# Where a graph layer's "own row" part is finished: at the first stage's store, or after the neighbour sums

## The chip, the cores and the metric

The kernel runs on one core of one Trainium2 chip. The metric is the device time of one launch in microseconds (us). The core has five engines that run side by side, each with its own in-order queue: TensorE (PE, with its weight loads shown as PEld), VectorE (DVE), ScalarE (ACT), GpSimd (POOL) and SyncE (SP, which here only issues transfers). They wait for each other through semaphores.

## The reference, cut to what matters

Four graph layers follow one another on x of 2708 x 512 numbers, each as `x = layernorm(x + layer(x, adj))`. The change touches the first layer alone:

```python
Ab   = A > 0                                   # A: 2708 x 2708
keep = Ab & (cumsum(Ab, axis=1) <= 64)         # the first 64 neighbours of each row
cnt  = keep.sum(axis=1, keepdims=True)
nb_mean = (keep @ X) / maximum(cnt, 1)
xj = leaky_relu(nb_mean @ W_nb.T + b_nb)       # neighbour part
xi = leaky_relu(X @ W_line.T + b_line)         # own part
out = xi + where(cnt > 0, xj, 0)
x1 = layernorm(x + out)                        # x of the next layer
```

The kernel computes `keep @ (X W_nb.T)` in place of `(keep @ X) W_nb.T`. leaky_relu is `max(0.01 u, u)`.

## The kernel before, in words

The 2708 rows are cut into 22 tiles: 21 of 128 rows and a last one of 20. A tile of x is 128 x 512 fp32, 256 KB.

**First stage** (the loop `for t in range(NT)`, up to 187 us in the profile). For each tile t, PE multiplies x(t), transposed, with W_nb (the first four matmuls of L299) and with W_line (the second four), two passes each. ACT and DVE split the first product into two parts, yH (L271) and yL (L276), whose sum the later matmuls use. DVE adds the bias to the second product (L451, tile `u`) and POOL issues the store of it to the array `r0_dram` (L452). So `r0_dram` holds `X W_line.T + b_line`, before the leaky step. The loads of x go over SP's queue (`fetched`, L205) into three buffers named `rows`; `early(k, ...)` issues them k tiles ahead of use.

Woven into the same loop is the work on 14 of the 22 row blocks of the adjacency: POOL issues the load of a block (L312, 677 KB), ACT counts its ones (L317, a sigmoid over 2708 columns), DVE finds the first 64 of each row in two parts, each a scan (L323) and a product (L326), and the block is then turned: every second one by a transposing transfer over SP's queue (L344) whose result ACT turns into the stored mask (L349), the others by PE (L335, ACT L339). `tc.issue_after(ins)` puts the instructions of its block behind `ins` on that engine: the load of the next adjacency block is put behind the store of the tile before (`stored[t - 1]`), the second part of `place` behind `low`, the last DVE instruction of the tile. The matmuls and transposes of this loop stand in a fixed order on PE (`pe`). The products lie in PSUM: one buffer each for `pm0` and `pm1`, and four buffers `acc` that the turning shares with every second product.

**Among the sums** (187 to 467 us). The tiles are summed in six groups, `cuts`: first the last two tiles (20, 21), then four at a time. For a group, PE runs over the 22 row tiles j (L608: the mask block kT times yH(j), yL(j)). kT is made by ACT one step ahead (L470, two buffers). ACT then scales the four sums into `u` (L621). The rest of a group is the generator `finish`, which is advanced during the next group's sums at the steps j that 3 does not divide (14 of 22), and in the last group's case once for each tile of the following loop. It adds the bias (L524), takes the leaky step (L229), fetches r0 and x (two `rows` buffers), takes the leaky step on r0 (L229 again, tile `rows`) and adds x (L528), adds the two parts (L530), normalises (L121 to L128, with one POOL instruction, L126), stores x1 (L532), and splits it into 16-bit words (L149, `store_words`) that are stored (L150) so that transposing transfers can load them turned (L155). The eight remaining adjacency blocks are counted, placed in four parts each (`other_masks`), and turned by L344 into ACT's L349 during the same sums, as steps of the generator `both`; they use the tiles `spare` and `w` in turn.

**The next layer's products** (467 to 625 us) repeat the first stage's pattern on x1: matmuls L299, yH, yL, bias add L642, and the mask rewritten by L636.

A scheduler orders the instructions of each engine, within the constraints named; SP's and POOL's queues are ordered by it too.

Of the kernel before, what the change touches and what calls it, by code (L numbers as in the profile page):

```python
# [16 lines left out]
OP = mybir.AluOpType  # L17
# [15 lines left out]
def kernel(  # L33
# [18 lines left out]
    def rows(t):  # L52
        return min(P, N - t * P)
# [183 lines left out]
    with ExitStack() as phase:  # L237
# [118 lines left out]
        with ExitStack() as ph:  # L356
            st = ph.enter_context(tc.tile_pool(name="l0a", bufs=1))
            wnT, wlT = weight(), weight2
            room = [maskT[:, G + k, :4 * D].bitcast(F32) for k in range(2 * KD)]

            fetches = []
            xs = early(2, NT, lambda t: fetched(x, t, rows(t), log=fetches))
            xTs = early(0, NT, lambda t, order=as_it_comes: transposed(ahead, ps_tr, xs(t), rows(t), "xT", order))

            warm = sums()
            for _ in range(8):
                pe(nc.tensor.matmul(warm[:, :P], ones, ones, start=True, stop=True))
            first_weights = list(transpose_weight(room[:KD], ps_tr, wnT, l0_w_nb, (nc.sync, nc.scalar)))  # L370
            line_weights = transpose_weight(room[KD:], ps_tr, wlT, l0_w_line)
            lows = {}
            xT = xTs(0, order=pe)
            lows[0] = keep_y(0, P, product(xT, P, wnT, 0, pe))
            xT = xTs(1, order=pe)
            weights_made = [next(line_weights) for _ in range(2)][0]
            pm = product(xT, P, wnT, 0, pe, sums())
            with tc.issue_after(list(line_weights)[-1].ins):
                lows[1] = keep_y(1, P, pm)
            b_line = bias(bcast(l0_b_line, D))  # L380
            def mask_tile():
                return st.tile([P, NT * P], BF16, name="m", bufs=3)

            def mask_rows(i):
                m = mask_tile()
                if i < 3:
                    with tc.issue_after(weights_made.ins):
                        nc.vector.memset(m[:, (0 if rows(turns[i]) < P else N - 1):], 0.0)
                else:
                    nc.gpsimd.memset(m[:, N:], 0.0)  # L390
                return load_mask(i, m)

            def by_dma(i):
                return i % 2 == 0 and i < HERE - 2

            def turned_tile():
                return end_tile(BF16)[:, :NT * P].rearrange("p (t n) -> p t n", n=P)

            masks = early(1, HERE, mask_rows)
            intos = {}  # L400

            def turn_next(i):
                if not by_dma(i):
                    for _ in turn_here(i, masks(i), lambda: sums(BF16, (P, G, P)), pe):
                        pass
                    return
                assert len(intos) < 2
                intos[i] = turned_tile()
                with tc.issue_after(fetches[-1].ins):
                    turn(i, masks(i), intos[i])  # L410
                due.append((t + 2, i))

            def signs_of(i, t):
                with tc.issue_after(highs[t].ins):
                    for _ in signs(i, intos.pop(i)):
                        pass
            masks(0)
            nc.gpsimd.memset(maskT[:, NT - 1, :], 0.0)
            nc.gpsimd.memset(maskT[:, :, N:], 0.0)
            counted = turned = 0  # L420
            due, stored = [], {}
            for t in range(NT):
                n = rows(t)
                if t == END:
                    assert not due and turned >= HERE - 2
                    ends[:] = [end_tile(F32R) for _ in range(2)]
                    for y in (yH, yL):
                        nc.gpsimd.memset(y(LAST).bitcast(F32), 0.0)
                if t > 1:

                    lows[t] = keep_y(t, n, product(xTs(t, order=pe), n, wnT, 0, pe, sums() if t % 2 else None))
                xT = xTs(t)
                if t + 1 < NT:
                    xTs(t + 1, order=pe)
                while due and due[0][0] <= t:
                    signs_of(due.pop(0)[1], t)
                while turned < min(HERE, counted - (t + 2 < NT and not by_dma(turned))):
                    turn_next(turned)
                    turned += 1
                now = counted < min(HERE, -(-t * HERE // (NT - 4)))  # L440
                if now:
                    with tc.issue_after(stored[t - 1].ins) if t > 2 else nullcontext():
                        m = masks(counted)
                    places = st.tile([P, N // 2], BF16, name="places", bufs=1)
                    with tc.issue_after(highs[t].ins), tc.issue_after(copied[0].ins):
                        count(counted, m)
                    with tc.issue_after(lows[t].ins):
                        place(counted, m, places, 0, 2)
                pm = product(xT, n, wlT, 1, pe, None if t % 2 else sums())
                u = sm.tile([P, D], F32, name="u")  # L450
                low = nc.vector.tensor_add(u[:n], pm[:n], b_line[:n])  # L451
                stored[t] = nc.gpsimd.dma_start(r0_dram[t * P:t * P + n, :], u[:n])  # L452
                if now:
                    with tc.issue_after(low.ins):
                        place(counted, m, places, 1, 2)
                    counted += 1
            with tc.issue_after(stored[LAST].ins):
                twins(0, turns[HERE - 1] + 1)
                twins(turns[0], NT)
# [3 lines left out]
        with ExitStack() as ph:  # L463
# [54 lines left out]
                nc.vector.reciprocal(one, one)  # L518

            def finish(ts_, us):  # L520
                for t in ts_:
                    n, u = rows(t), us[t]
                    r0, x0 = fetched(r0_dram, t, n), fetched(x, t, n)
                    nc.vector.tensor_add(u[:n], u[:n], b_nb[:n])  # L524
                    leaky(u[:n], u[:n])
                    with tc.issue_after(low.ins):
                        leaky(r0, r0)
                        nc.vector.tensor_add(r0, r0, x0)  # L528
                    yield
                    nc.vector.scalar_tensor_tensor(u[:n], u[:n], has[:n, t:t + 1], r0, op0=OP.mult, op1=OP.add)  # L530
                    layer_norm(sm, u[:n], n, u[:n])
                    nc.gpsimd.dma_start(x1_dram[t * P:t * P + n, :], u[:n])  # L532
                    store_words(r0 if ts_ == range(*cuts[-1]) else words, x1_words, t, u)
                    yield

# [1100 lines left out]
```

## Time and profile before

| what | us |
| --- | --- |
| median of 3 runs | 2882.63 (2882.36 to 2885.61) |
| the profiled execution | 2884.27 |
| its span from first to last instruction | 2882.5 |
| PE busy in it | 2806.0 (97%) |
| DVE busy | 2008.4 (70%) |
| ACT busy | 1525.4 (53%) |
| POOL busy | 267.1 (9%) |

The profile is one execution. A line such as "L608 PE MATMUL acc<-yH,kT" names the source line, the engine, the operation and the tiles, output first. "Idle before" is time in which the engine stood still just before that instruction, with what released it. The times of the timeline count from the start of the span. One instruction's time includes its latency: two instructions of one engine can overlap by a little, so the distance from start to start is what a further instruction costs on a busy engine. PEclk is the granted TensorE clock, 1.0 being full speed.

### The profile page before, as it was taken

The numbers are of one execution on the slowest core, as the hardware profiler recorded it, in microseconds if no ns is written. First come the engines' busy times: TensorE is split into PE (matmuls) and PEld (weight loads), VectorE is DVE, ScalarE is ACT, GpSimd is POOL, SyncE is SP. The second block draws the span as 40 slices with busy tenths as digits, with TensorE's granted clock in tenths as the row PEclk, the third lists the DMA queues.
The fourth block names the chain that finished last, engine by engine and source line by source line (L and its number), as shares of the span: only waits on it lengthen the run. The fifth ranks groups of instructions, "written<-read, shape, count | busy, mean of one in ns | idle before, by whom it ended". The sixth has DMA issues, their size and how long they took to land. (4 is left out here: it accounts for less than half of the span.)

```text
span 2882.5 us, 35707 instructions
## 1 busy us (share of the span) xinstructions
PE 2806.0 (97%) x13910; PEld 1553.3 (54%) x13910; DVE 2008.4 (70%) x2386; ACT 1525.4 (53%) x1749; POOL 267.1 (9%) x436
## 2 busy tenths in 40 slices
PE   9999999999999999999999999999999999999998
PEld 5457665458887433444466433444375555555565
DVE  7867747543436999999978999999954435445242
ACT  4646533223335999999955999999951000000011
POOL 2112110111110000000021000000200010100001
PEclk9999999999999999999999999999999999999999
DMA  7746647424323011111152111111161000000000
GB/s 172 154 98 135 148 128 189 129 76 123 106 87 75 28 37 37 35 55 38 36 167 94 38 38 41 50 42 34 36 162 62 4 26 15 26 15 16 15 15 28
DMA packets 203668, 202.64 MB, mean 70 GB/s; under 512 B 126837, under 2 KB 151738, under 8 KB 203490
## 3 DMA queue, kind: packets, MB, share of 16 engines
q1 hardware_dynamic: 170646, 127.60, 16.7%
q0 software_dynamic: 21840, 68.46, 8.1%
q10 hardware_dynamic: 11004, 4.22, 0.6%
q8 instruction: 111, 1.82, 0.3%
q14 instruction: 67, 0.55, 0.1%
HBM read 137.90 MB, written 55.66 MB: 67 GB/s over the span
## 5 line engine op out<-in xcount | busy, mean ns | idle before, releaser
L866 DVE SCALAR_TENSOR_TENSOR e<-v_bc,ucol,maskT 128x1408 f32<-128x1408 f32 (+3 forms) x798 | 1132.5, 1479 | 316.4 <-PE pn L1267 308.4
L895 ACT ACTIVATE c<-e,bcol 128x1300 fp8e4<-128x1300 f32 (+2 forms) x688 | 956.5, 1412 | 61.6 <-DVE e L866 16.2
L1067 PE MATMUL po<-e,R 128*64 128x512 f32 (+3 forms) x4224 | 894.0, 548 | 25.4 <-DVE e L866 23.1
L1067 PEld LDWEIGHTS po<-e,R 128*64 128x64 f32 (+1 forms) x4224 | 333.9, 136 | 552.5 <-issue 389.4
L1267 PE MATMUL pn<-e,R 128*128 128x512 f32 (+1 forms) x1008 | 396.3, 557 | 0.7
L1267 PEld LDWEIGHTS pn<-e,R 128*128 128x128 f32 x1008 | 177.5, 190 | 195.9 <-issue 181.2
L1196 ACT ACTIVATE w<-pl,b 128x256 f32<-128x256 f32 (+1 forms) x88 | 41.0, 466 | 365.6 <-PE pl L1194 365.6
L126 POOL TENSOR_TENSOR ln_rs<-ln_rs,half 128x1 f32<-128x1 f32 (+1 forms) x88 | 54.3, 617 | 1320.3 <-DVE ln_rs L125 1311.3
L608 PE MATMUL acc<-yH,kT 128*128 128x512 f32 x418 | 169.9, 407 | 5.7 <-ACT kT L470 4.8
L787 PE MATMUL pm<-w,xT 128*128 128x264 f32 (+1 forms) x704 | 164.0, 388 | 4.1 <-DVE R L805 1.5
L608 PE MATMUL acc<-yL,kT 128*128 128x512 f32 x418 | 163.4, 391 | 0.0
L658 PE MATMUL acc<-yH,mf 128*128 128x512 f32 x418 | 162.7, 389 | 0.0
L658 PE MATMUL acc<-yL,mf 128*128 128x512 f32 x418 | 162.6, 389 | 0.0
L1194 PE MATMUL pl<-lin 128*128 128x256 f32 (+1 forms) x704 | 152.9, 371 | 0.6 <-DVE lin L1096 0.6
L1219 PE MATMUL pl<-lin,w 128*128 128x512 f32 x336 | 150.8, 593 | 0.0
L1194 PEld LDWEIGHTS pl<-lin 128*128 128x128 f32 x704 | 129.3, 190 | 31.2 <-issue 15.8
L787 PEld LDWEIGHTS pm<-w,xT 128*128 128x128 f32 (+1 forms) x704 | 129.7, 190 | 29.7 <-ACT xT L141 4.2
L655 ACT CAST mf<-maskT 128x1024 fp32r<-128x1024 fp8e4 (+1 forms) x66 | 64.5, 978 | 148.5 <-PE acc L658 143.9
L299 PE MATMUL pm<-w,xT 128*128 128x512 f32 x288 | 130.1, 594 | 3.5 <-DVE yL L276 2.7
L470 ACT ACTIVATE kT<-maskT 128x512 fp32r<-128x512 fp8e4 (+1 forms) x132 | 77.6, 593 | 99.0 <-PE acc L608 98.8
L967 PE MATMUL pd<-c,parts_c 128*12 128x384 fp8e4 (+2 forms) x2688 | 128.3, 307 | 0.0
L299 PE MATMUL pm<-weight,xT 128*128 128x512 f32 (+1 forms) x256 | 117.1, 600 | 1.5 <-DVE u L642 1.5
(280 smaller groups left out, 2773.4 us busy)
## 6 DMA issues: line engine op xcount, KB each, us to landing
v_bc<-v_dram SPq DMA_DIRECT2D x16, 704.0 KB
rows<-in_x_dram SPq DMA_DIRECT2D x42, 256.0 KB
x_dram<-u POOLq DMA_DIRECT2D x42, 256.0 KB, 2.6
v_bc<-v_dram SPq DMA_DIRECT2D x16, 650.0 KB
m<-in_adj_dram POOLq DMA_DIRECT2D x13, 677.0 KB, 7.7
r_dram<-u POOLq DMA_DIRECT2D x21, 256.0 KB, 3.6
rows<-r_dram SPq DMA_DIRECT2D x21, 256.0 KB
z_dram<-u POOLq DMA_DIRECT2D x21, 256.0 KB, 2.6
```

The source lines that it names most:

```text
L299: order(nc.tensor.matmul(pm[:m], xT[:, k, :m], w[:, k, :], start=(k == 0), stop=(k == KD - 1)))
L470: made = nc.scalar.activation(kT[:, :w], maskT[:, j, b[0] * P:b[0] * P + w], AF.Relu, scale=-1.0)
L608: nc.tensor.matmul(pa[t], kT[:, (t - b[0]) * P:(t - b[0] + 1) * P], y(j), start=(j == 0 and y is yH), stop=(j == LAST))
L658: nc.tensor.matmul(pa, mf[:, j - g0, :], y(j), start=(j == 0 and y is yH), stop=(j == LAST))
L787: nc.tensor.matmul(pm[a][:m, :D // 2 + heads], xT[:, k, :m], w[:, k, a, :D // 2 + heads], start=(k == 0), stop=(k == KD - 1))
L866: self.made = nc.vector.scalar_tensor_tensor(e[:, :w], v[:, :w], ucol[:, j, h:h + 1], maskT[:, j, c0:c0 + w], op0=OP.max, op1=OP.mult)
L895: nc.scalar.activation(c[:, :w], e[:, :w], AF.Sigmoid, bias=bcol[:, j, h:h + 1], scale=STEP, saturate=False)
L967: pe(nc.tensor.matmul(p[32 * g:32 * g + 12, :c1 - c0], parts_c[:, j, h, :], c[:, c0:c1], start=(i == 0 and h == hs[0]), stop=(i == NT - 1 ...
L1067: pe(nc.tensor.matmul(po[i][HO * k:HO * k + HO, :c1 - c0], R2[at, j, h * HO:(h + 1) * HO], e[at, a:a + c1 - c0], start=(i_ == 0), stop=(i_ ...
L1194: nc.tensor.matmul(pl[:, :w], self.lin1[:, k, f * P:(f + 1) * P], h[:, k, :w], start=(k == 0), stop=(k == KD - 1))
L1219: nc.tensor.matmul(pl[:n], gT[:, f, (t - t0) * P:(t - t0) * P + n], self.lin2[:, f, :], start=(f == 0), stop=(f == KF - 1))
L1267: nc.tensor.matmul(pn[k][:, :w], R2[at, j, k * P:(k + 1) * P], e[at, :w], start=(j == 0), stop=(j == NT - 1))
```

## The change

In the first stage, the leaky step is taken on `u` right after the bias add, on DVE, in place; POOL adds the tile of x to it; then it is stored. So `r0_dram` holds `x + leaky_relu(X W_line.T + b_line)`. `low` now names the leaky step. The x tile is used once more, after its transposition, and the loads of x are issued one tile ahead of `xs` in place of two.

In `finish`, x is no longer fetched, and the leaky step on r0 and the add of x (L528) are gone. r0 is fetched one tile ahead within the group. The instruction that adds the two parts comes under `issue_after(low.ins)`, after a `yield`; and there is a third `yield` in each tile, between the normalisation with its store and `store_words`. A group of four tiles thus takes 12 steps where it took 8. In the last group the words are written into the r0 tile, as before.

```diff
-            xs = early(2, NT, lambda t: fetched(x, t, rows(t), log=fetches))
+            xs = early(1, NT, lambda t: fetched(x, t, rows(t), log=fetches))
...
                 u = sm.tile([P, D], F32, name="u")
                 low = nc.vector.tensor_add(u[:n], pm[:n], b_line[:n])
+                low = leaky(u[:n], u[:n])
+                nc.gpsimd.tensor_add(u[:n], u[:n], xs(t))
                 stored[t] = nc.gpsimd.dma_start(r0_dram[t * P:t * P + n, :], u[:n])
...
             def finish(ts_, us):
-                for t in ts_:
-                    n, u = rows(t), us[t]
-                    r0, x0 = fetched(r0_dram, t, n), fetched(x, t, n)
+                r0s = early(1, len(ts_), lambda i: fetched(r0_dram, ts_[i], rows(ts_[i])))
+                for i, t in enumerate(ts_):
+                    n, u, r0 = rows(t), us[t], r0s(i)
                     nc.vector.tensor_add(u[:n], u[:n], b_nb[:n])
                     leaky(u[:n], u[:n])
+                    yield
                     with tc.issue_after(low.ins):
-                        leaky(r0, r0)
-                        nc.vector.tensor_add(r0, r0, x0)
-                    yield
-                    nc.vector.scalar_tensor_tensor(u[:n], u[:n], has[:n, t:t + 1], r0, op0=OP.mult, op1=OP.add)
+                        nc.vector.scalar_tensor_tensor(u[:n], u[:n], has[:n, t:t + 1], r0, op0=OP.mult, op1=OP.add)
                     layer_norm(sm, u[:n], n, u[:n])
                     nc.gpsimd.dma_start(x1_dram[t * P:t * P + n, :], u[:n])
+                    yield
                     store_words(r0 if ts_ == range(*cuts[-1]) else words, x1_words, t, u)
                     yield
```

## The prediction

> **What bounds the kernel now.** PE is busy 97% of the span, so only its idle time and its clock can move the end. I cut the part that the change touches by stage (the table of windows; columns: time and, for PE, PEld, DVE, ACT and POOL, us busy and instructions; then PEclk, DMA share, GB/s):
>
> ```profile
> 28.40:95.00 66.60, 62.95 (x224) 30.93 (x223) 62.72 (x50) 37.84 (x53) 8.82 (x18) 0.97 0.72 149
> 95.00:169.50 74.50, 74.06 (x274) 37.09 (x273) 63.61 (x51) 46.16 (x60) 11.29 (x23) 1.00 0.68 143
> 169.50:187.40 17.90, 17.90 (x67) 7.80 (x65) 4.05 (x7) 5.06 (x10) 2.94 (x7) 1.00 0.34 83
> 187.40:219.00 31.60, 25.26 (x96) 16.60 (x96) 20.46 (x22) 17.22 (x31) 3.65 (x9) 1.00 0.42 93
> 219.00:467.00 248.00, 238.67 (x963) 178.74 (x964) 159.71 (x264) 124.67 (x190) 44.92 (x71) 0.98 0.57 144
> 467.00:535.00 68.00, 63.69 (x145) 26.70 (x144) 57.30 (x91) 15.74 (x19) 12.30 (x21) 1.00 0.61 170
> ```
>
> In the first 67 us of the adjacency work DVE idles 3.9 us, less than anything beside PE: it is as full as PE. From 187 us it is not. Then the waits, for what PE lost: of PE before 187 us (first line), of PE from 187 to 535 us (next three), of ACT among the sums (last); columns: total us, times, longest.
>
> ```profile
> PE acc L335 <- DVE u L451: 3.6, 1, 3.6
> ...
> PE acc L608 <- ACT kT L470: 13.1, 12, 3.3
> PE pm L299 <- DVE yL L276: 2.7, 2, 2.3
> PE pm L299 <- DVE u L642: 1.5, 1, 1.5
> ...
> ACT maskT L349 <- DMA weight<-spare: 12.4, 3, 5.1
> ```
>
> PE's one long stall of the first stage (at 89.4 us) is DVE's backlog: the buffer that PE needs was read by L451 only after a scan. Among the sums, three of PE's twelve stalls are long: 2.75 us at 216, 2.23 at 300, 3.30 at 347. Each time ACT had no kT ready because it stood, in order, behind L349, which waited 3.2, 4.1 and 5.1 us for a turned adjacency block. That transfer starts when DVE ends the block's last L326.
>
> Two of these stalls cost more than their gap (windows around 347, 300 and 89 us):
>
> ```profile
> 343.00:354.00 11.00, 7.70 (x22) 5.14 (x20) 8.47 (x14) 7.26 (x12) 0.53 (x1) 0.69 0.45 156
> 296.00:306.00 10.00, 7.56 (x25) 5.28 (x24) 6.66 (x7) 5.97 (x10) 1.45 (x3) 0.83 0.67 155
> 86.00:97.00 11.00, 7.57 (x19) 3.58 (x19) 9.23 (x7) 4.96 (x8) 1.36 (x4) 0.84 0.53 114
> ```
>
> Clock lost, (1 - PEclk) x window: 11 x 0.31 = 3.4 us, 10 x 0.17 = 1.7, 11 x 0.16 = 1.8. At 216 us nothing was lost.
>
> **What the Trainium skill says.** (1) "TensorE: Matmul & The Clock Gate", section "What's actually happening": after an idle window of about 3.4 us TensorE falls to half speed, and needs a busy window to return. The trace agrees on the loss (1.7 us is half of 3.4), but a gap of 2.23 us was enough. (2) "GPSIMD Engine Reference", section 8, "Key points": GpSimd shares its SBUF interfaces with VectorE, "contention with DVE instructions in a 2-port perf mode or with two SBUF inputs". (3) Same page, section 3.1: a GpSimd add of two tensors takes about twice VectorE's time. On (2) and (3) the trace has a case, the same kind of add late in the kernel (timeline of POOL, of DVE there, of DVE elsewhere; columns: start, us):
>
> ```profile
> 2644.34 1.30 POOL L1190 TENSOR_TENSOR rows<-rows,b 128x512 f32<-128x512 f32 x1
> ...
> 2644.55 1.64 DVE L1244 SCALAR_TENSOR_TENSOR acc<-e,ecol,acc 128x512 f32<-128x512 f32 x1
> ...
> 2568.93 0.75 DVE L1244 SCALAR_TENSOR_TENSOR acc<-e,ecol,acc 128x512 f32<-128x512 f32 x1
> ```
>
> The add takes 1.30 us (DVE's adds: 0.68), and the DVE instruction beside it 0.89 us longer than elsewhere. At 2760.54 a DVE instruction begun before the add took 1.62 us in place of 0.37: 1.25 more. So DVE stands still for about one microsecond per add.
>
> **The change, part by part.**
>
> *Leaky step in the first stage.* 22 instructions on DVE of 0.68 us; start to start it is 0.60 (L229 at 204.71, next at 205.31). *Add on POOL.* 22 of 1.30 us, 29 us; POOL is busy 8.8 of 66.6 us there, so its own time is hidden. Its price is DVE's standing still: no row shows it beside a scan. Lower bound 0 (a scan takes 3.0 us for 1354 columns, so it might leave room; where DVE idles it also costs nothing), upper 1.25; I take 1.0, since three kinds of DVE instruction (L866, L1242, L1244) all showed 0.88 or more and a scan too reads two SBUF tiles. So 1.6 us per tile.
>
> From 28.4 to PE's stall at 89.4 us seven tiles (1 to 7) come with it: 7 x 1.6 = 11.2 us, against 3.0 us of idle (DVE's wait for ACT's count before the scan at 68.6) that fill first. PE waits 8.2 us more; as that is more or longer stalls, I add one more clock loss, 1.7: +9.9. From 95 to 169.5 us: ten tiles, 16.0 us, against 10.9 us of idle. 6.3 of that idle is waiting for ACT's counts, which may move along, so half is used, 5.5. Of the 10.5 left, about 5 is late work that runs into the light tail (DVE busy 4.05 of 17.9 us), where PE needs little of it: +5. First stage: **+15**. Low end: adds cost nothing, 7 x 0.6 - 3.0 = +1. High end, 1.85 a tile: 10 + 3.4 and 13: +26.
>
> *x one tile ahead, and held until the add.* Three buffers stay. The load of x(t+3) now waits for POOL's add of t: after L451(t) come L326 0.85, leaky 0.60, perhaps a scan 3.0, the add 1.3, the load 3 (a load of this size landed 2.9 us after its issue): 8.8 us. PE turns x(t+3) two tiles later; with 0.6 us of transposes and 3.6 us of product the loop takes 13 us of two tiles' 16. Zero in the estimate. SP's transposes L344 stand two x loads earlier in the changed order, and x loads behind a late one are needed two tiles on: zero too. POOL's store comes 0.6 + 1.3 us later or more, and behind it in order the adjacency load: see rival 1.
>
> *Among the sums.* DVE loses L229 and L528 on `rows`: 22 x 2 x 0.60 = 26 us, of the 180 busy from 187 to 467 us, so hidden except where an L326 comes sooner. SP loses 22 loads (256 KB each, 5.8 MB at some 144 GB/s); nothing but DVE's own waits (40.5 and 17.3 us for r0 and x) hung on them. The three stalls: at 216, the block's first scan waited for r0 of tile 21 and two instructions (200.48, while the count ended 199.1), and one L229 lies between: 1.4 + 0.6 = 2.0 sooner, gain 2.0 of 2.75. At 300: L528 twice and L229, L530 and L121 leave the stretch between first scan and transfer, while L149 and L123 enter or stay; interleaved work falls from some 4.2 to 1.8 us, 2.4 sooner; the stall of 2.23 goes, with its clock loss: 3.9. At 347: the same, 2.4 of 3.3, and the clock loss 3.4: 5.8. Late next there: the scans' own count on ACT, which leaves 0.2 us stalls. Sum: **-11.7**. Least: 2, if the words below hold L326 up. Most: -14.
>
> *Words a step later, r0 one ahead.* In the changed order the last L149 of a group stands before the last L326 of the block. L149 writes the single `words` tile, so it waits for the store before: 7.9 us from L149 to L149 when slow (269.4 to 277.3), 4.3 when not. I take the latter, then it is ready in time: 0. The steps, 12, fit in 14. In the last group r0 holds two of the three `rows` buffers for 12 tiles, so turned words get one: joining copy 1.16 + transfer about 3.3 = 4.5 us per tile of 6.9: hidden.
>
> *Next layer's products, 467 to 535 us.* PE waits 2.3 and 1.5 us for DVE, busy 57.3 of 68. Eight instructions go, 4.8 us, but mask rewriting and `wa` stay ahead of L642: **-1.5**.
>
> Sum: +15 - 11.7 - 1.5 = +1.8 on the profiled execution's 2884.27 (span 2882.5 and 1.8 around it): 2886. The median of the runs shown is 1.6 lower, so I say **2885**. 0.2% is 5.8 us, about what a measurement of this kernel can tell from no change: the forecast is no change, two large parts of opposite sign. Its own range: 2878 to 2893.
>
> **Rivals.**
>
> *1. Slower: the adjacency load comes late.* POOL's order is add, store, clear, load; the load lands 7.7 us after issue and is counted one tile (8.0 us) later; ACT already waited 6.2 us for it. If the store slips by 0.6 + up to 3.0 + 1.3 = 4.9 us, so does each of 11 loads, and ACT keeps yH and xT behind the count. It decides once the slip exceeds DVE's backlog. Half of it through to PE: 11 x 2.4 = 27, less the 10 already counted as DVE's: +17 on the sum, about 2902; a third: 2893. Against: ACT's wait is hidden while DVE is still behind.
>
> *2. Slower: L326 is held up by the words.* Then the sums give 2 in place of 11.7: 2895. For: L149 did wait 8.3 us in total. Against: four times only.
>
> *3. Faster: adds fall in scans or idle time.* The first stage costs +1 to +4, the rest stays: 2871 to 2876. For: at 2643.76 a DVE instruction that had begun before an add was not slowed. Against: DVE idles 3.9 of 66.6 us.
>
> *4.* That x1 is ready sooner changes nothing: the next layer's products begin with tiles that were stored long before.
>
> **How the numbers follow.** Forecast 0.37 (of it 0.30 within 0.2%, 0.07 slower), rival 1 0.20, rival 2 0.14, rival 3 0.29 (of it 0.27 faster, 0.02 within). Faster 0.27, same 0.32, slower 0.41. Range 2870 to 2901.
>
> **What would show it.** Right: L1244-like stretching of L323 or L229 beside POOL's new add, by about 1 us; DVE above 95% from 28 us to the last L326, which ends 10 us or more later than 168.7; PE waiting for L451 or L276 there for more than 10 us; the waits of L349 for `spare` below 4 us in sum, and PEclk 1.0 around 300 and 347 us. Wrong: scans at 3.0 us beside the adds (rival 3); ACT's L317 waiting for the adjacency load for over 15 us (rival 1); L149 waiting ahead of L326 (rival 2).

## The result, and the profile after

The changed kernel takes 2906.3 us in the median (2895.6 to 2912.1, 8 runs) against 2883.6 (2882.2 to 2887.8, 8 runs) for the kernel before on the same chip: ratio 1.0071, 95% interval 1.0056 to 1.0086. It is slower by 0.7%, and lies above the forecast's range, which ended at 2901. The profiled execution took 2906.27 us, its span 2904.4.

In the changed kernel the bias add is still L451, the leaky step is shown as L229, the GpSimd add is L453, the store L454, the matmuls of the sums L609 and their kT L472. Cut at the first L609, the last L609 and the first matmul of the layer after:

| us | before | after | difference | predicted |
| --- | --- | --- | --- | --- |
| first stage | 187.4 | 226.1 | +38.7 | +15 |
| sums | 277.9 | 264.9 | -13.0 | -11.7 |
| next layer's products | 157.0 | 155.2 | -1.8 | -1.5 |
| the rest | 2260.3 | 2258.1 | -2.2 | 0 |

So the whole miss lies in the first stage. The rest differs by as much between kernels whose code there is the same (2255.3 to 2260.7 us with the changed `finish`). The next layer's products take 153.4 to 155.7 us with the changed `finish` in all runs below, 157.0 and 157.2 (e4) with that of before: a small gain that is there. The table of windows of the kernel after (columns as before: the window and, for PE, PEld, DVE, ACT, POOL, us busy and instructions; then PEclk, DMA share, GB/s):

```profile
28.40:66.00 37.60, 33.15 (x105) 15.44 (x104) 36.69 (x30) 16.15 (x24) 19.64 (x12) 0.95 0.56 106
28.40:95.00 66.60, 48.70 (x161) 23.29 (x160) 48.26 (x40) 26.55 (x37) 27.65 (x20) 0.87 0.67 103
95.00:206.00 111.00, 99.38 (x342) 49.93 (x340) 95.94 (x81) 58.69 (x79) 48.52 (x38) 0.94 0.62 126
206.00:226.10 20.10, 18.10 (x62) 7.98 (x62) 5.33 (x8) 4.98 (x10) 6.47 (x11) 0.92 0.36 89
226.10:491.00 264.90, 257.05 (x1054) 191.94 (x1054) 157.93 (x250) 140.57 (x217) 52.64 (x82) 1.00 0.53 130
491.00:561.00 70.00, 66.29 (x155) 29.03 (x154) 50.37 (x76) 17.97 (x23) 11.29 (x18) 1.00 0.58 153
```

The second row is the window of the prediction's first row. In it PE is down from 62.95 to 48.70 us, and DVE, which was to become fuller, is down too: 48.26 of 66.6 us, 72%. The first row cuts this window at 66 us. Up to there DVE is as full as was forecast, 36.69 of 37.6 us, 98%; behind it both engines stood waiting for something else. POOL is up by 18.8 us over the second row, where the six adds that fall in this window would be 7.8 at 1.3 us each. The fifth row is the gain that was forecast: PEclk 1.00 through all of the sums.

The waits of the kernel after (total us, times, longest): PE's largest before 226 us, SP's queue there, then PE and ACT behind 226 us:

```profile
PE ps_tr L139 <- DMA rows<-in_x_dram: 31.1, 9, 13.4
...
SPq L205 <- POOL u L453: 145.9, 16, 21.5
...
PE acc L609 <- ACT kT L472: 5.8, 10, 1.6
PE pm L299 <- DVE yL L276: 2.4, 1, 2.4
PE pm L299 <- DVE u L643: 1.3, 1, 1.3
...
ACT maskT L349 <- DMA weight<-spare: 1.9, 2, 1.5
```

PE now waits nine times for tiles of x, for which no wait is listed before, and SP's queue waits 16 times for the GpSimd add: the load of x at its head needs the buffer that the add still reads. Among the sums, kT's lateness fell from 13.1 to 5.8 us, and L349's wait for `spare` from 12.4 to 1.9.

The longest of the nine waits, in the timelines of SP, POOL and PE (start, us):

```profile
57.75 0.33 SPq L205 DMA_DIRECT2D rows<-in_x_dram  x1
58.51 10.04 SPq L344 DMA_TRANSPOSE end<-m  x1
68.72 0.46 SPq L205 DMA_DIRECT2D rows<-in_x_dram  x1
...
58.02 0.58 POOL L454 DMA_DIRECT2D r_dram<-u  x1 [0.30 <-POOL u L453]
58.72 0.74 POOL L312 DMA_DIRECT2D m<-in_adj_dram  x1
...
81.49 0.90 PE L139 MATMUL ps_tr<-ident,rows 128*128 128x128 f32 x3 [13.44 <-DMA rows<-in_x_dram]
```

One add ends at 57.7 us. It releases a load of x on SP (57.75) with the transposing transfer behind it (58.51), and on POOL the store (58.02) with the adjacency load behind it (58.72). The two large transfers start within 0.21 us of each other. The transposing one holds SP's queue for 10.04 us, where the one at 55.0 us of the kernel before held it for 5.01. The next load of x goes out at 68.72 and PE has its rows at 81.49, 12.8 us later; the load issued at 38.07 us was used at 41.38.

In the packet records of the two traces the transposing transfer's 256-byte packets took 18 ns in the median when it ran alone (before, 78 to 82 us); from 62 to 78 us after, the medians of 2 us slices lie between 18 and 234 ns. All its packets took from 60.5 to 79.9 us, nearly twice as long as it held SP's queue (before: 56.2 to 62.3 us). The Trainium skill, "DMA: Bandwidth & Descriptors", section "Queues, rings and completion order", says that each DMA engine takes turns between the queues that it has work for, packet by packet. The records fit that: packets of SP's and of GpSimd's queue started in every microsecond from 61 to 79 us. It does not say that the turns cost this much, and no run here shows why they do.

PE's idle time from 20 us to the end of the first stage is 31.8 us after and 4.1 before; its busy time there rose from 163.3 to 174.3, because the waits cost clock as well (PEclk 0.92 over those 206 us against 0.99 over 167). 27.7 and 11.0 make the 38.7. The Trainium skill, "TensorE: Matmul & The Clock Gate", section "What's actually happening", gives an idle window of some 3.4 us as what halves the speed; here gaps of 2.2 us were enough (the one at 208.0 us was followed by 3.4 us at half clock), as in the kernel before.

### The profile page after: what moved, and what is told of

The parts are those of the page before. It is cut to its first block, busy times and chain, and to the rows that moved or that the text cites. A ratio compares the mean times of both kernels' runs of the same rounds, so it can differ in the third digit from the quotient of the medians.

```text
span 2904.4 us, 35657 instructions
## 1 busy us (share of the span) xinstructions
PE 2809.6 (97%) x13910; PEld 1557.8 (54%) x13910; DVE 2002.7 (69%) x2364; ACT 1526.6 (53%) x1749; POOL 332.2 (11%) x458
## 3 DMA queue, kind: packets, MB, share of 16 engines
q1 hardware_dynamic: 167592, 122.05, 16.2%
## 5 line engine op out<-in xcount | busy, mean ns | idle before, releaser
L896 ACT ACTIVATE c<-e,bcol 128x1300 fp8e4<-128x1300 f32 (+2 forms) x688 | 956.6, 1412 | 61.6 <-DVE e L867 16.4
L609 PE MATMUL acc<-yH,kT 128*128 128x512 f32 x418 | 169.9, 407 | 6.8 <-ACT kT L472 4.8
L609 PE MATMUL acc<-yL,kT 128*128 128x512 f32 x418 | 163.4, 391 | 0.0
L1195 PEld LDWEIGHTS pl<-lin 128*128 128x128 f32 x704 | 129.5, 190 | 31.0 <-issue 15.8
L299 PE MATMUL pm<-w,xT 128*128 128x512 f32 x288 | 129.7, 593 | 3.0 <-DVE yL L276 2.4
L472 ACT ACTIVATE kT<-maskT 128x512 fp32r<-128x512 fp8e4 (+1 forms) x132 | 77.7, 594 | 99.6 <-PE acc L609 99.2
L299 PE MATMUL pm<-weight,xT 128*128 128x512 f32 (+1 forms) x256 | 120.7, 616 | 1.3 <-DVE u L643 1.3
```

What stands on the lines that cost most here:

```text
L299: order(nc.tensor.matmul(pm[:m], xT[:, k, :m], w[:, k, :], start=(k == 0), stop=(k == KD - 1)))
L472: made = nc.scalar.activation(kT[:, :w], maskT[:, j, b[0] * P:b[0] * P + w], AF.Relu, scale=-1.0)
L609: nc.tensor.matmul(pa[t], kT[:, (t - b[0]) * P:(t - b[0] + 1) * P], y(j), start=(j == 0 and y is yH), stop=(j == LAST))
L896: nc.scalar.activation(c[:, :w], e[:, :w], AF.Sigmoid, bias=bcol[:, j, h:h + 1], scale=STEP, saturate=False)
L1195: nc.tensor.matmul(pl[:, :w], self.lin1[:, k, f * P:(f + 1) * P], h[:, k, :w], start=(k == 0), stop=(k == KD - 1))
```

## The experiments

The end of the first stage is the start of the first matmul of the sums. It repeats to about 4 us between kernels that ought to agree, as e4 shows. "Ratio" is to the kernel before, run beside it, with its 95% interval. The kernels of e2, e6 and e7 leave x out of the first layer's sum. Stages are those of the one profiled execution, ratios those of all runs. The theories have letters in the expectations: H, the buffer of x held until the add; C, the transposing transfer and the adjacency load going out together; M, the GpSimd add beside VectorE's work costing in itself (in e1 alone, M is the adjacency load coming late behind the store); D, P, V and L are named where they come.

**e4: only the look-ahead.**

```diff
 (kernel before)
-            xs = early(2, NT, ...)
+            xs = early(1, NT, ...)
```

> The kernel before with x loaded one tile ahead in place of two, nothing else; buffers come free at the transposes. If the shorter look-ahead alone makes x late, PE waits over 10 us for x in the first stage and the time is 2895 or more. If it needs the held buffer too (theory H), PE waits under 4 us for x and the time is 2881 to 2888.

Ratio 0.9999 (0.9990 to 1.0008), first stage 191.1 us. One tile ahead costs nothing by itself: there a buffer is free as soon as its tile is turned.

**e2: no add.**

```diff
 (kernel after)
-            xs = early(1, NT, ...)
+            xs = early(2, NT, ...)
...
                 low = leaky(u[:n], u[:n])
-                nc.gpsimd.tensor_add(u[:n], u[:n], xs(t))
```

> The changed kernel without GpSimd's add (x is left out of the first layer's sum), and with x loaded two tiles ahead; three buffers, each free after its transposes as before. The leaky step and all of finish as changed. Theory H: the first stage ends within 6 us of before's 187.4 and the time is 2868 to 2876. Theory D: the leaky step alone gives VectorE 0.6 us a tile, so the first stage ends between 190 and 198 us, 2875 to 2882. The difference to the run with four buffers is what the add itself costs where x is not late.

Ratio 0.9961 (0.9947 to 0.9975), first stage 190.1, sums 265.3 us. So the leaky step costs no more of the first stage than kernels differ by anyway (190.1 - 187.4 = 2.7 us), the gain among the sums is real, and the add with what hangs on it costs 36.0 us (226.1 - 190.1). All later runs ask what of the add does it.

**e3: the add on VectorE, behind the scan.**

```diff
-                nc.gpsimd.tensor_add(u[:n], u[:n], xs(t))
+                nc.vector.tensor_add(u[:n], u[:n], xs(t))
```

> The changed kernel with the add of x taken by VectorE in place of GpSimd; three x buffers held until the add, one tile ahead, as changed. Theory H with GpSimd's slow add as its cause (3.9 us beside a scan): the buffer comes free about 1 us sooner at best, since the add now stands behind the same scan on VectorE, but the adds no longer stretch L326; x is still late, PE waits 15 to 30 us for it, 2890 to 2905. If GpSimd sharing VectorE's way to memory is itself the cause: PE's waits for x fall below 8 us, 2870 to 2882.

Ratio 1.0074 (1.0056 to 1.0091), first stage 214.9 us, PE's waits for rows 21.4 us. The scheduler put the add behind the second scan, so it ended as late as on GpSimd. Taking GpSimd out of it did not make the kernel faster: the ratio is that of the kernel after. (The profiled execution, 2897.1 us, is near the fastest of its four; their median is 2899.9.) This is what theory H expected.

**e1: a fourth x buffer, and two tiles ahead.**

```diff
-            xs = early(1, NT, lambda t: fetched(x, t, rows(t), log=fetches))
+            xs = early(2, NT, lambda t: fetched(x, t, rows(t), *((st, "x4", 1) if t % 4 == 3 else ()), log=fetches))
```

> The changed kernel with a fourth x buffer in the first stage (every fourth tile of x in a buffer of that stage's own pool) and x loaded two tiles ahead again; the leaky step on VectorE and GpSimd's add stay. Theory H (the x buffer is held until the add, so x comes late): PE's waits for x, 31 us with 34 us at half clock in the changed kernel, fall below 8 us; the first stage ends near 195 us in place of 226, and the time is about 2875 (2868 to 2882). Theory D (VectorE is overloaded by the leaky step and the add beside it): the waits go over to L451 and L276, the first stage ends after 212 us, and the time is 2893 or more. Theory M (the adjacency loads come late behind the store): ACT's L317 waits over 20 us, the time is 2890 or more.

Ratio 1.0067 (1.0050 to 1.0084), first stage 224.0 us: no gain. PE's many waits of 2 to 4 us for rows are gone, but one of 15.4 us stays. The transfer of L344 went out at 58.11 us, the adjacency load at 58.3, and SP's queue stood for 15.4 us. So held buffers alone are not the cause. (This profiled execution is the slowest of four: 2906.9 us, median 2901.2.)

**e5: the add on VectorE, ahead of the scan.**

```diff
-                low = leaky(u[:n], u[:n])
-                nc.gpsimd.tensor_add(u[:n], u[:n], xs(t))
+                leaky(u[:n], u[:n])
+                low = nc.vector.tensor_add(u[:n], u[:n], xs(t))
```

> The add runs on VectorE between the leaky step and the second scan, and the scan is told to follow the add. Nothing is left out. Theory P (the place of the add costs: it ends 4 to 5 us late because of the scan, and with it the release of the x buffer, the store and the next adjacency load): PE's waits for rows in the first stage fall from 31 us to under 5, no transposing transfer of L344 takes over 6 us, the first product of the sums starts near 193 us instead of 226, and the time is 2872 to 2877 us. Rival V (an extra 1.3 us of VectorE per tile, or holding the buffer at all, is what costs): no better than the add on VectorE behind the scan, 2895 to 2900 us.

Ratio 1.0003 (0.9994 to 1.0012), first stage 207.7 us. The place matters: 7.2 us better than behind the scan (e3). But neither theory's number was met. PE still waits six times for rows, 12.3 us in all, the longest 2.0, 5.0 and 3.5, and one transfer takes 7.1 us.

**e6: x held, nothing else late.**

```diff
 (kernel of e2, early(1); behind the second scan, on one column)
+                nc.vector.tensor_add(probe[:n], u[:n, :1], xs(t)[:, :1])
```

> The kernel without the add (x left out of the sum), looking one tile ahead, and x(t) held until behind the second scan by a VectorE step that reads one column of it; the store and the adjacency load behind it stay early. Theory H+C (a held x buffer and a late store each cost): x waits of 2 to 4 us per tile come back, some 17 us of gaps and some 8 us of clock, and the time is 2870 + 15 to 25, 2885 to 2895 us; the transposing transfers stay under 6 us. Theory C alone (only the collision of the adjacency load with the transposing transfer costs): 2870 to 2874 us.

Ratio 1.0041 (1.0026 to 1.0056), first stage 212.0 us, 21.9 more than without the hold. Waits of PE in the first stage:

```profile
PE ps_tr L139 <- DMA rows<-in_x_dram: 16.4, 6, 4.7
```

A step that costs next to nothing itself, but reads one column of x late, brings the waits for rows back. This is what theory H+C expected, and theory C alone is ruled out.

**e7: the store late, x not held.**

```diff
 (kernel of e2)
-                stored[t] = nc.gpsimd.dma_start(r0_dram[...], u[:n])
                 if now:
...
                         place(counted, m, places, 1, 2)
                     counted += 1
+                nc.vector.tensor_copy(u[:n, :1], u[:n, :1])
+                stored[t] = nc.gpsimd.dma_start(r0_dram[...], u[:n])
```

> The kernel without the add (x left out of the sum), looking two tiles ahead, x not held; a VectorE step on one column of u behind the second scan makes the store, and the adjacency load behind it on GpSimd's queue, as late as in the changed kernel. Theory H+C: the transposing transfer of L344 near 57 us goes out beside the adjacency load and takes over 8 us, PE waits 10 to 15 us once for rows behind it, and the time is 2870 + 13 to 22, 2883 to 2892 us. Theory H alone (only the held x buffers cost): 2870 to 2874 us.

Ratio 0.9987 (0.9980 to 0.9994), first stage 198.9 us, 8.8 more than e2. Its waits in the first stage:

```profile
ACT m L317 <- DMA m<-in_adj_dram: 14.4, 4, 4.5
...
PE acc L335 <- DVE m L326: 5.2, 2, 4.1
PE acc L299 <- ACT maskT L339: 3.5, 1, 3.5
...
PE ps_tr L139 <- DMA rows<-in_x_dram: 0.6, 1, 0.6
```

The transfer took 10.3 us, as both transfers were 0.45 us apart, but PE hardly waited for rows, as two tiles of x lay ready. What the late store cost went another way: the adjacency load behind it came late, so did the count, the product L326 and the turned mask. The expected 13 to 22 us were too many, and the wait for rows was the wrong one.

**e8: only the leaky step moved; x is loaded and added in `finish`.**

```diff
 (kernel of e2)
-                    n, u, r0 = rows(t), us[t], r0s(i)
+                    n, u, r0, x0 = rows(t), us[t], r0s(i), fetched(x, t, rows(t))
...
                     with tc.issue_after(low.ins):
+                        nc.vector.tensor_add(r0, r0, x0)
                         nc.vector.scalar_tensor_tensor(u[:n], u[:n], has[:n, t:t + 1], r0, op0=OP.mult, op1=OP.add)
```

> Only the leaky step is moved into the first stage; x is loaded in finish, beside the own rows that are loaded one tile ahead, and added there on VectorE. Nothing is left out. Theory H+C: the first stage is that of the kernel without the add (first product of the sums at 190 us), the 22 adds of 1.26 us among the sums lie beside TensorE, and the time is 2870 to 2875 us. If the gain among the sums came from the single load per tile, the stalls for rows there return and it is 2878 to 2884 us.

Ratio 0.9983 (0.9974 to 0.9991): faster than both kernels. First stage 190.8, sums 271.0 us. Waits among its sums:

```profile
DVE rows L529 <- DMA rows<-in_x_dram: 17.2, 6, 8.6
...
PE acc L609 <- ACT kT L471: 11.0, 13, 2.3
```

With the load and add of x back, the sums give 6.9 of the 13.0 us, so the other 6 hang on having one load per tile and no add. The first stage came as expected, the total 3 us higher.

**e9 and e10: a fourth buffer, one tile ahead,** so that x(t+2) goes into the buffer of x(t-2). e9 is the kernel after with it, e10 the kernel of e5.

```diff
-            xs = early(1, NT, lambda t: fetched(x, t, rows(t), log=fetches))
+            xs = early(1, NT, lambda t: fetched(x, t, rows(t), *((st, "x4", 1) if t % 4 == 3 else ()), log=fetches))
```

> The changed kernel with the fourth x buffer, but still looking one tile ahead: x(t+2) goes into the buffer of x(t-2), whose add is long done, so SP's queue is not held; the GpSimd add and the late store stay. Nothing is left out. Theory H+C (held queue and late store, nothing else): the first stage is that of the late store alone, 199 us, plus up to 4 us, the first product of the sums near 199 to 203 us, the time 2878 to 2884 us; no x load is issued together with an add's end. Rival M (the GpSimd add beside VectorE's scans costs in itself, by stretching VectorE's steps): the first product of the sums stays beyond 212 us, the time 2892 us or more.

e9: ratio 1.0050 (1.0035 to 1.0066), first stage 219.6 us, by the number rival M's. But PE's longest loss was one wait behind one transfer, not VectorE's steps; its waits for rows in the first stage:

```profile
PE ps_tr L139 <- DMA rows<-in_x_dram: 13.2, 1, 13.2
```

That transfer held SP's queue 16.2 us, with the adjacency load 0.2 us behind it. The expectation that no load of x is issued at an add's end was wrong too. SP runs ahead until a buffer is missing, so it always stands at some add, and the transfer behind it still goes out with the store and the adjacency load.

> As the one before, and the add on VectorE ahead of the second scan, so that neither the queue is held nor the store late. Nothing is left out. Theory H+C: the first stage is that of the kernel without the add, 190 us, plus 1 to 4 us for 1.26 us more of VectorE per tile; sums 265 us; the time is 2869 to 2874 us, ratio to before near 0.996. Rival V (VectorE's 1.26 us per tile lie on the path): first product of the sums beyond 200 us, the time 2878 us or more.

e10: ratio 0.9990 (0.9984 to 0.9997), first stage 200.9 us. By the numbers rival V is right, though narrowly (200.9 against 200, 2878.9 against 2878): with waits for rows down to 0.9 us and no transfer above 5.4 us, 10.8 us over e2 remain, with 1.26 us more of VectorE per tile. PE waits for VectorE's and ACT's late mask work:

```profile
PE acc L335 <- DVE m L326: 4.5, 2, 2.5
PE acc L335 <- DVE u L451: 3.2, 1, 3.2
PE acc L299 <- ACT maskT L339: 2.2, 1, 2.2
```

**e11 and e12: the transposing transfer a little later.** e11 is the kernel after with this edit, e12 that of e9.

```diff
-                with tc.issue_after(fetches[-1].ins):
-                    turn(i, masks(i), intos[i])
+                held.append(i)
...
                 stored[t] = nc.gpsimd.dma_start(r0_dram[t * P:t * P + n, :], u[:n])
+                while held:
+                    i = held.pop()
+                    mt, r = masks(i), rows(turns[i])
+                    with tc.issue_after(low.ins):
+                        nc.vector.tensor_copy(mt[:r, :1], mt[:r, :1])
+                    turn(i, mt, intos[i])
```

> The changed kernel whole, with one thing moved: the transposing transfer of L344 is held for some 5 us, until behind the next tile's leaky step, so that it goes out well behind the adjacency load of L312 instead of 0.2 us ahead of it. Nothing is left out; the held x loads stay as they are. Theory C (the two transfers started together slow each other, and the x load behind them is late): the transfer near 64 us takes under 6 us of SP's queue, PE's longest wait for rows falls from 13.4 to 3 to 6 us, the first product of the sums starts at 208 to 214 us instead of 226, and the time is 2888 to 2894 us. Rival (the long wait comes from the held x load or the GpSimd add, whatever the transfers): the longest wait stays over 10 us and the time 2900 us or more.

e11: ratio 1.0037 (1.0024 to 1.0050), first stage 213.0 us in place of 226.1. Timelines of POOL and SP:

```profile
58.14 0.73 POOL L312 DMA_DIRECT2D m<-in_adj_dram  x1
59.33 8.35 SPq L344 DMA_TRANSPOSE end<-m  x1
```

The transfer moved by 0.8 us only, not by 5, but from 0.2 us ahead of the adjacency load to 1.2 us behind it. PE's longest wait for rows fell from 13.4 to 5.4 us. The first stage is the one that theory C expected, and its rival is ruled out; but the transfer still takes 8.35 us, not under 6, and the median, 2895.1 us, lies one above the range set. The gain is not in the time on SP's queue, 8.35 for 10.04, but in the packets: the transfer's last one ends at 71.7 us in place of 79.9, and the load of x, issued at 67.84 in place of 68.72, is used at 73.14 in place of 81.49. With 1.2 us of lead the adjacency load's packets were through by 66 us, and most of the transfer's came behind them.

> The same move of the transposing transfer in the kernel with the fourth x buffer and one tile ahead; the GpSimd add stays where it is, nothing is left out. Theory H+C (held x buffers and coincident transfers are all of the loss): the first product of the sums falls from 219.6 to 198 to 204 us and the time from 2896.6 to 2876 to 2882 us. Rival M (the GpSimd add beside the scans costs in itself, through VectorE's and GpSimd's later steps): the first product stays beyond 208 us, 2886 us or more.

e12: ratio 1.0015 (1.0006 to 1.0024), first stage 206.5 us, between the two expectations; the median, 2888.8 us, is in the range of rival M. Waits for rows are 1.1 us. What is left:

```profile
ACT m L317 <- DMA m<-in_adj_dram: 17.3, 4, 6.1
...
PE acc L335 <- DVE m L326: 6.8, 3, 4.7
PE acc L299 <- ACT maskT L339: 5.4, 1, 5.4
PE acc L335 <- DVE u L450: 2.8, 1, 2.8
```

These are the waits of e7, somewhat longer. Beside them ACT waits 14.0 us for turned blocks (L349; 4.3 in e7): the later transfer has its own price.

**e13: meant to put the adjacency load ahead of the add** on GpSimd's queue, in the kernel of e9.

```diff
+            def finished():
+                for t, n, u, x_t in late:
+                    nc.gpsimd.tensor_add(u[:n], u[:n], x_t)
+                    stored[t] = nc.gpsimd.dma_start(r0_dram[t * P:t * P + n, :], u[:n])
+                late.clear()
...
-                    with tc.issue_after(stored[t - 1].ins) if t > 2 else nullcontext():
+                    with tc.issue_after(stored[t - 2].ins) if t > 3 else nullcontext():
                         m = masks(counted)
+                    finished()
...
-                nc.gpsimd.tensor_add(u[:n], u[:n], xs(t))
-                stored[t] = nc.gpsimd.dma_start(r0_dram[t * P:t * P + n, :], u[:n])
+                late.append((t, n, u, xs(t)))
```

> The kernel with the fourth x buffer and one tile ahead, with each GpSimd add and its store moved behind the next step's adjacency load on GpSimd's queue, instead of ahead of it; the add still runs on GpSimd, nothing is left out. So neither a held x buffer nor a late adjacency load is left, and the transposing transfer goes out some 3 us behind the adjacency load; only the GpSimd add itself stays. Theory L (of the 16 us that were left with the fourth buffer and the later transfer, the late adjacency load is most): the first product of the sums falls from 206.5 to 192 to 199 us, ACT's waits for the adjacency load fall from 17 us to under 10, and the time is 0.994 to 0.998 of before. Rival M (the GpSimd add beside VectorE's scans costs in itself): the first product stays beyond 203 us and the time at 1.000 or more of before.

Ratio 1.0074 (1.0056 to 1.0091), first stage 228.9 us. Most adjacency loads now stood behind the add and store of the tile before (the load at 58.12 us behind the add that ends at 57.14), so the order that L needs was mostly not made. ACT's waits for the adjacency load did fall to 5.8 us, as L said, but PE waited 21.9 us for rows meanwhile, so this says nothing of what they cost. But the new order made the two transfers coincide three times in place of once (timelines of SP and POOL):

```profile
57.93 13.60 SPq L344 DMA_TRANSPOSE end<-m  x1
58.12 0.73 POOL L312 DMA_DIRECT2D m<-in_adj_dram  x1
...
94.57 3.23 SPq L344 DMA_TRANSPOSE end<-m  x1
...
114.05 13.96 SPq L344 DMA_TRANSPOSE end<-m  x1
114.26 0.73 POOL L312 DMA_DIRECT2D m<-in_adj_dram  x1
...
150.14 3.36 SPq L344 DMA_TRANSPOSE end<-m  x1
...
169.63 13.21 SPq L344 DMA_TRANSPOSE end<-m  x1
169.84 0.73 POOL L312 DMA_DIRECT2D m<-in_adj_dram  x1
```

Each of the three is followed by a wait of PE for rows, 9.4, 4.0 and 8.5 us; the transfers between them take 3.2 to 3.4 us.

All 90 transposing transfers of the first stages of the fifteen kernels, by the start of the nearest adjacency load:

| adjacency load against the transfer | transfers | the transfer holds SP's queue, us |
| --- | --- | --- |
| none within 5 us | 37 | 3.2 to 5.2 |
| 1.4 to 4.6 us behind | 28 | 3.3 to 5.3 |
| 0.1 to 0.2 us behind (after, e1, e3, e9, three times in e13) | 7 | 8.9 to 16.2 |
| 0.5 us ahead (e7) | 1 | 10.3 |
| 1.1 to 1.2 us ahead (e6, e11, e12) | 3 | 6.2 to 8.4 |
| 3.2 to 4.8 us ahead | 14 | 3.3 to 7.1 |

So a transfer that has 1.4 us of lead is hardly slowed, and one that starts with the load, at whatever time of the stage, is.

## Why the prediction was wrong, and where it was right

**The step that failed** is "*x one tile ahead, and held until the add*", "Zero in the estimate", with its second zero, for SP's transposes. Its loop was put at 8.8 us from L451 plus 4.2 of PE, 13 of two tiles' 16. The kernel after shows one turn of it: x(4) takes the buffer of x(1) (timelines of DVE, SP and PE; the first line is L451 of tile 1, the last that of tile 3):

```profile
32.00 0.67 DVE L451 TENSOR_TENSOR u<-pm,bias 128x512 f32<-128x512 f32 x1
...
38.07 0.34 SPq L205 DMA_DIRECT2D rows<-in_x_dram  x1
...
41.38 1.09 PE L139 MATMUL ps_tr<-ident,rows 128*128 128x128 f32 x4 [2.78 <-DMA rows<-in_x_dram]
42.26 4.75 PE L299 MATMUL pm<-weight,xT 128*128 128x512 f32 x8
...
48.79 2.96 DVE L323 TENSOR_TENSOR_SCAN places<-m,over 128x1354 bf16<-128x1354 bf16 x1
51.67 0.66 DVE L451 TENSOR_TENSOR u<-pm,bias 128x512 f32<-128x512 f32 x1
```

From L451 to the rows in use it is 9.4 us for the 8.8 counted. PE's part, to the end of tile 3's second product at 47.0, is 5.6 for 4.2, as PE had waited and its clock was halved from 41.15 to 44.56 us. Then tile 3's L451 stands behind VectorE's work on the mask, a scan last, for another 4.7 us, which the loop put at nothing. In all it is 19.7 us, more than the 16. Part of that is VectorE's own pace, as it was 98% busy there. The second zero missed more: what stands behind the held load on SP was not costed as released by the same add as the store and the adjacency load on POOL. The prediction looked at each queue for its own lateness, not at two queues being let go at one moment.

| | transfer as in after | transfer later |
| --- | --- | --- |
| three buffers | 226.1 (after) | 213.0 (e11) |
| four buffers | 219.6 (e9) | 206.5 (e12) |

First stages in us: the fourth buffer saves 6.5 in both columns, the later transfer 13.1 in both rows, together 19.6. A stage repeats to about 4 us only, so that the sums agree so closely is chance; but the medians of all runs, each less that of the kernel before beside it, say nearly the same: 22.7 (after), 10.2 (e11), 15.8 (e9) and 3.9 (e12), so 6.3 to 6.9 for the one and 11.9 to 12.5 for the other. Where the 13.1 arise is not the same either: with four buffers 12.3 of them come at the one tile behind the transfer, with three some 8, and the rest bit by bit behind it. Left after both is 206.5 - 187.4 = 19.1, against the +15 of the sum. So the two terms set to zero make most of the stage's miss, 19.6 of 23.7 us. That the rest is near what was counted is partly luck: it holds the late store (8.8 us alone, e7) and a transfer that is still slow (8.2 us), neither of which the sum counted. The size of one cause depends on what else is late: holding alone costs 21.9 us (e6). Taking it away from the kernel after brings 6.5: PE's waits for rows fall from 31.1 to 13.2 us, but its waits for the turning of the masks and the PSUM buffers it uses (L335 and L299, for L326, L339 and L451) rise from 0.2 to 15.3 (e9).

**The add beside VectorE** was put at 1.0 us of VectorE's time each, 0 to 1.25. The timelines of POOL and DVE (start, us):

```profile
25.53 1.26 POOL L453 TENSOR_TENSOR u<-u,rows 128x512 f32<-128x512 f32 x1 [3.56 <-DVE u L229]
34.12 3.92 POOL L453 TENSOR_TENSOR u<-u,rows 128x512 f32<-128x512 f32 x1 [6.44 <-DVE u L229]
...
32.58 0.85 DVE L326 TENSOR_TENSOR m<-m,places 128x1354 bf16<-128x1354 bf16 x1
33.95 3.03 DVE L323 TENSOR_TENSOR_SCAN places<-m,places,over 128x1354 bf16<-128x1354 bf16 x1
37.48 1.29 DVE L326 TENSOR_TENSOR m<-m,places 128x1354 bf16<-128x1354 bf16 x1
...
186.08 1.30 POOL L453 TENSOR_TENSOR u<-u,rows 128x512 f32<-128x512 f32 x1
186.62 3.60 DVE L323 TENSOR_TENSOR_SCAN places<-m,over 128x1354 bf16<-128x1354 bf16 x1 [0.68 <-ACT m L317]
```

In 13 of the 22 tiles the add begins some 0.17 us behind the start of a scan. It then takes some 3.9 us in place of 1.26 and ends 1.1 us after the scan each time, and the scan takes its usual 3.0: it is the add that is held up. Only the product behind the scan is longer, 1.29 for 0.85 (twice 1.75). VectorE so loses 0.4 us, twice 0.9, not 1.0; instead everything behind the add is 2.7 us later. Once, at 186 us, the add began first: then it kept its time and the scan took 3.60, the stretching that was forecast. The contention that the Trainium skill names ("GPSIMD Engine Reference", section 8) is there; which side pays was wrong in all but this one case. Of the other signs, VectorE was over 95% busy up to 66 us only, and PE did not wait for L451 or L276. The sign set for rival 3, scans of 3.0 us beside the adds, did come, but not its time, as it left out that the add itself becomes late.

**Rival 1**, the late adjacency load, is part of the rest. ACT waited for it 9.1 us after, below the 15 set, but 17.3 us where the waits for rows were gone (e12) and 20.0 where one was left (e9); a late store alone costs 8.8 us (e7). **Rival 3** (2871 to 2876) names what a free add would have given: e2, which has none, is 0.9961 of before, some 2871 us. **Rival 2** did not occur: L149 waited 11.8 us in all, but L349's wait for `spare` was 1.9, so L326 was in time.

**The sums** gave -13.0 for -11.7, in the main by the steps named: the stalls at 300 and 347 us and their clock losses are gone, the one of 2.75 us at 216 is down to 1.0. A wait that was not counted is gone too, 1.7 us of PE for the tile that L560 writes. That x's loads hung on nothing was wrong, e8 says: they with their add cost about 6 us. **The next layer's products** gave -1.8 for -1.5, but not by the stalls named, which are still there (2.4 and 1.3 us); so the agreement is luck, and where the gain came from was not followed.

**Still open:** of the 16.4 us by which e12 exceeds e2, the late store explains up to the 8.8 of e7. Whether the rest is the add's hold on VectorE's products, the still later adjacency loads, or the transfer that was moved (8.2 us on SP's queue, ACT's 14.0 us behind it) no run tells apart. Why two transfers that start together take so long is not shown either.

## What to carry to other kernels

Before another reader is given to a buffer, count from the moment its new last reader ends to the moment the next tile is needed, in the order that the consumer really follows, and then list everything that stands behind that release on every queue: here one late add let go two large transfers at once. A cheap instruction put on an idle engine is not free where it must wait for a long one beside it; putting it ahead of the long one gave back the loss (e5, 1.0003 of before) and, with a fourth buffer, a little more (e10, 0.9990); putting it into a later stage with room gave the fastest complete kernel here (e8, 0.9983). And where two large transfers come free together, it is worth giving one of them a lead: 1.2 us of lead took 13 us off the stage, with the same bytes moved (e12 against e9).

## What was not expected of the hardware

- A transposing transfer and a 677 KB load started within 0.5 us of each other: the transfer held SP's queue for 8.9 to 16.2 us (8 cases), against 3.2 to 5.3 with no such load within 5 us or with the load 1.4 us or more behind it (65 cases). With the load 3.2 to 4.8 us ahead it is 3.3 to 7.1.
- A GpSimd add of two 128 x 512 fp32 tiles that begins 0.17 us after a VectorE scan ends 1.1 us after the scan (3.92 us in place of 1.26), and the scan is not slowed (13 cases). Where the add began 0.54 us before the scan, the scan took 3.60 us in place of 2.97 and the add its usual 1.30 (one case).
